# Two groups of four batches, re-laid expert weights and a folded local gate in a two-layer kernel

## The chip, the cores and the metric

The kernel runs on one core of a Trainium2 chip. The time is that of the device for one execution, in microseconds (us). The five engines are named as in the profile: PE (TensorE, with its weight loads as PEld), DVE (VectorE), ACT (ScalarE), POOL (GpSimd) and SP (SyncE, which here only issues transfers).

## The reference, cut to what matters

Eight batches of 512 tokens, 128 channels wide, go through two layers. Each layer adds an attention and a mixture of experts to its input.

```python
xn = layernorm(x)
x = x + L0_attn(xn) + L0_ffn(xn)        # states of two key sets; 8 experts, the best one
xn = layernorm(x)
x = x + L1_attn(xn) + L1_ffn(xn)
```

Layer 0's attention forms for each of two key and value projections a state over all tokens, `einsum('kbhnd,kbhne->kbhde', ks, vs)`, multiplies the two states, and applies the queries to the product.

Layer 1's attention has a local part (windows of 32 keys and the 32 before, 16 heads) and a remote part (64 latents), each with a gate that depends on the query:

```python
base = (j > i) & (j <= i + W)            # i: query in its block, j: key in its window of 64
sc = where(mask, einsum(Qb, Kw) / sqrt(D), -inf)
local = einsum(softmax(sc), Vw)
gl = sigmoid(einsum('bhsd,hd->bhs', Q, gate_local_w))
gr = sigmoid(einsum('bhsd,hd->bhs', Q, gate_remote_w))
out = (gl * local + gr * rem) @ w_out
```

By `base`, key 0 of a window is seen by no query.

Layer 1's experts send each token to two of eight:

```python
logits = x_flat @ gate_w.T
topk_probs, topk_idx = top_k(softmax(logits), 2)
hidden = relu(einsum('th,ehf->tef', x_flat, w1) + b1)   # F = 512
y = einsum('tef,efh->teh', hidden, w2) + b2
y_flat = sum(gathered(y, topk_idx) * topk_probs)
```

## The kernel before

All work is float32. Every product has therefore two instructions ("passes") on PE. A batch is 4 tiles of 128 tokens.

*Stages.* `layer0(b)` (line 756) does layer 0 for a batch and also projects `v` and the logits of layer 1. `attention1(b)` (line 923) is layer 1's attention. `route(h)` (line 1152) sorts the tokens of a group of batches by expert; `experts1(h)` (line 1309) runs the experts over the group's tiles; `output(b)` (line 1431) fetches the expert rows back and adds them.

*Groups.* `GROUPS = (2, 3, 3)` at line 34 says how many batches share a routing. Each token counts twice, and each expert's rows are rounded up to tiles of 128, so a group of n batches has `_tiles(n)` = (1024 n + 1016) // 128 tiles at most, all of which are run: 23, 31 and 31.

*An expert tile.* SP loads `w1`, `w2` (256 KB each) and `b2` of the tile's expert. POOL gathers its 128 rows from DRAM (`xgt`), PE transposes them (`tpx`), four products give `hp` (line 1405), ACT adds the bias and applies relu (`ht`), four products give `yp`, DVE adds `b2` (`ys`) and POOL scatters the rows (`y_rows`, line 1371). The bias comes out of a small product of `b1r` (line 580) with the one-hot expert of each tile.

*Layer 0's experts.* The gate of each token is written to DRAM as `gd` and read back for each expert, broadcast to all partitions (`gbc`, line 704); DVE and POOL in turn multiply it with the input (`xg`), and PE sums eight products into `rp`.

*Layer 0's states.* For each key set, `hk` (line 822) is a sum of four products with the keys as the stationary operand; ACT copies it, PE transposes it (`tph`), ACT copies that to `hT`.

*Layer 1's local part.* Queries of four heads at a time are spread into `qe`, keys lie in `kT` (line 939) with 32 zeros ahead, and a product for each block and each four heads gives scores against a window of 64 keys (`sc`, line 1076). For each pair of score banks ACT copies the past keys to `m`, DVE lays the seen own keys over it (predicated copy), then maximum (`amx`), difference, exponential, sum (`asd`), reciprocal (`ard`, line 1110) and the division follow, a transpose (`pt`), two masks (`pw`), and the products into `pv`. The gates come from two 512-column products (`gj`) and two tanh into `gsb` (line 988); the local one is applied in `loc` (line 1139), and POOL adds it to `aT`.

*The order.* No engine call is issued where it stands. A `Recorder` (line 126) collects every operation with an estimated duration (`_duration`, line 395) and with its dependencies; `order` (line 238) then places them on the engines' timelines, by rank, and each engine's instructions are issued in that order. The ranks come from `PLAN` (line 1461), a start and an end for every stage and batch, found by the authors and written out by hand. `_fill` (line 349) puts bf16 products of zeros into pauses that the plan expects on PE. All recorded operations carry the line of the recorder's call, 389, so the profile tells them apart by tile names.

Of the kernel before, what the change touches and what calls it, by code (L numbers as in the profile page):

```python
# [33 lines left out]
GROUPS = (2, 3, 3)  # L34
# [39 lines left out]
def _constants():  # L74

    c = np.zeros((P, _CN), np.float32)
    p = np.arange(P)

    def put(name, a):
        lo, hi = _CCOL[name]  # L80
        c[: a.shape[0], lo:hi] = a.reshape(a.shape[0], hi - lo)

    put("ident", np.eye(P))

    less = np.eye(P)
# [12 lines left out]
    g = np.arange(P // CHUNK)  # L98
    late = np.zeros((P, P), np.float32)
    group = np.zeros((P, P), np.float32)  # L100
    for at in (0, LC):
        late[at : at + len(g)] = np.where(p[None, :] % len(g) > g[:, None], NEG, 0.0)
        group[at : at + len(g)] = p[None, :] // CHUNK == g[:, None]
    put("late", late)
    put("group", group)
    put("first", np.broadcast_to(E - np.arange(E), (P, NT, E)))
    put("before", p[:, None] < p[None, :])
    put("iota", np.broadcast_to(p, (P, P)))
    put("part4", p[:, None] // NFC)
    put("chunk4", p[:, None] % NFC == np.arange(NFC)[None, :])  # L110
    put("within", p)
    n = 2 * max(GROUPS) * NT
    put("tile", np.broadcast_to(1 + np.arange(n), (P, n)))
    return c


class Op:
# [4 lines left out]
        "missing", "opens", "claims", "index", "follows", "shape", "last", "room",  # L122
# [3 lines left out]
class Recorder:  # L126
# [8 lines left out]
    PAUSE, FILL = 0.6, 0.8  # L135
    filled = 0
# [23 lines left out]
    def add(self, engine, emit, writes, reads, time, delay, shape=None):  # L160
# [12 lines left out]
        op = Op()  # L173
        op.engine, op.emit, op.time, op.delay = engine, [emit], time, delay
        op.shape = op.last = shape
        op.index, op.follows = len(self.ops), ()
        op.uses = uses
        self.ops.append(op)
# [59 lines left out]
    def order(self):  # L238
# [26 lines left out]
        free = dict.fromkeys(("PE", "DVE", "ACT", "POOL", "SP"), 0.0)  # L265
        shape = None
# [7 lines left out]
        while len(out) < len(self.ops):  # L274
# [47 lines left out]
            free[e] = op.end  # L322
            for t in uses.get(op.index, ()):
                left[t.name] -= 1
                holders[t.name] = max(holders.get(t.name, 0.0), op.end + op.delay)
                if not left[t.name]:
                    slots[t.tag].append(holders[t.name])
            for other in op.before:
                lag = op.delay
# [39 lines left out]
class _Engine:  # L369
# [3 lines left out]
    def __getattr__(self, method):  # L373
# [3 lines left out]
        def record(*args, **kwargs):  # L377
# [6 lines left out]
            if name == "tensor":  # L384
                rows = aps[1].shape[0]
                cols = int(np.prod(list(aps[1].shape)[1:])) if method == "matmul" else P
                shape = (rows, 32 * ((cols + 31) // 32))
            r.add(
                r.ENGINES[name], lambda: call(*args, **kwargs), aps[:1], aps[1:], time, delay, shape  # L389
# [5 lines left out]
def _duration(engine, method, aps):  # L395
# [6 lines left out]
    if "dma" in method:  # L402
        size = 4e-6 * int(np.prod(list(aps[0].shape)))
        return (1.25, 2.4) if engine == "gpsimd" else (0.5, 2.0 + 5.0 * size)
# [18 lines left out]
    if method == "reciprocal":  # L423
# [5 lines left out]
        0.095 + (0.28 if len(aps) == 4 and (n == P or n < 8) else 0.0)  # L429
# [6 lines left out]
def two_layers_kernel(  # L436
# [52 lines left out]
    experts_row = work.tile([1, E * C], F32, tag="gsb", name="experts_row", bufs=1)  # L489
# [66 lines left out]
    wgl = const.tile([P, 2, P], F32, name="wgl")  # L556
    nc.vector.tensor_scalar_mul(wgl[:, 0], ct("heads"), wt("gl"))
    nc.vector.tensor_scalar_mul(wgl[:, 1], ct("heads"), wt("gr"))
# [18 lines left out]
    nc.gpsimd.memset(vb, 0.0)  # L577

# [31 lines left out]
    nc.scalar.copy(b1r, b1p[: E * NFC, :P])  # L610
# [103 lines left out]
    for h, n in enumerate(GROUPS):  # L714
# [17 lines left out]
        "hk": "w2",  # L732
# [23 lines left out]
    def layer0(b):  # L756
# [77 lines left out]
        hT = tile(work, [P, 2, C], "hT", "hT" + nm)  # L834
        nc.scalar.copy(hT, tp[:, : 2 * C].rearrange("p (k c) -> p k c", c=C))
# [75 lines left out]
    wgl1 = const.tile([P, 2, P], F32, name="wgl1")  # L911

    def gates_of_input():
# [6 lines left out]
        mm(wp[:, : 2 * P], wqT, wgl.rearrange("p k c -> p (k c)"))  # L920
        nc.scalar.copy(wgl1.rearrange("p k c -> p (k c)"), wp[:, : 2 * P])

    def attention1(b):
# [64 lines left out]
        gsb = work.tile([P, 2, N], F32, tag="gsb", name="gsb" + nm, bufs=1)  # L988
# [63 lines left out]
        nc.vector.scalar_tensor_tensor(aT, gsb[:, 1, :], 1.0, rem_p, ALU.add, ALU.mult)  # L1052
# [21 lines left out]
        for hf in range(2):  # L1074

            four = [bank(f"sc{nm}_{hf}{r}") for r in range(4)]
            with nc.together(0.31):
                for j in range(8):
                    blk = 8 * hf + j
                    for r in range(4):  # L1080
# [228 lines left out]
    def experts1(h):  # L1309
# [6 lines left out]
        def fetch(j):  # L1316
# [29 lines left out]
            for move, to in ((load_first, first), (load_second, second), (load_third, third)):  # L1346
                nc.add("SP", move, [to], [], 0.55, 3.3)
                nc.ops[-1].follows = (fetch.last,)
# [17 lines left out]
        def scatter(j, ys):  # L1366
# [8 lines left out]
            nc.add("POOL", store, [], [ys, ids], 1.25, 2.4)  # L1375
# [21 lines left out]
        for j in range(TILES + 1):  # L1397
            if j < TILES:
# [53 lines left out]
    def load_next(b):  # L1452
        xs[b] = load_x(b)
        if b == 1:
# [13 lines left out]
        "attention1": (  # L1468
            (33, 150), (148, 194), (204, 270), (284, 611),
            (549, 789), (924, 1084), (1023, 1271), (1198, 1498),  # L1470
        ),
        "experts1": ((68, 410), (427, 1006), (967, 1293)),
        "output": (
            (676, 701), (627, 663), (1181, 1203), (995, 1107),
            (1262, 1379), (1408, 1425), (1456, 1524), (2493, 2506),
# [80 lines left out]
```

## Time and profile before

| | |
|---|---|
| median of 8 runs | 616.31 us (613.77 to 618.62) |
| the profiled execution | 616.91 us |
| its span, first to last instruction | 614.9 us |
| mean granted TensorE clock | 0.965 |
| DMA bytes moved | 91.63 MB, 106,532 packets |
| expert tiles | 85 |

A row of a profile names an engine, the operation, the tile that it writes and those it reads, with the shape, the count, the busy time, the mean of one, and the idle time of the engine ahead of it with what ended that. Busy time of overlapping instructions is counted once.

### The profile page before, as it was taken

How to read it: one execution, taken by the hardware profiler on the slowest of the kernel's cores; microseconds unless marked ns; L12 is line 12 of the kernel's file. 1: busy time of each engine (PE TensorE's matmuls, PEld its weight loads, DVE VectorE, ACT ScalarE, POOL GpSimd, SP SyncE). 2: the span in 40 equal slices, each digit the busy share in tenths (PEclk: the TensorE clock that was granted, in tenths of full speed). 3: DMA queues.
4: the chain of work that ended last, by engine and by line, in shares of the span. 5: the costliest groups of instructions: out<-in, count | busy, mean ns of one | idle time of the engine just before them, and what ended most of it. 6: DMA issues, size and time to landing. Idle time of an engine off the chain costs nothing.

```text
span 614.9 us, 15660 instructions
## 1 busy us (share of the span) xinstructions
PE 550.3 (89%) x5487; PEld 455.0 (74%) x5487; DVE 478.1 (78%) x1297; ACT 343.3 (56%) x950; POOL 402.8 (66%) x422
## 2 busy tenths in 40 slices
PE   9989888889989899879998979987998999999893
PEld 3478577679778578757987868987777888888842
DVE  2796899988979889997866868789843773965695
ACT  3623737653856775445677438454585468557620
POOL 3045134689578738844776877887778898887562
PEclk9999999889999999989997989989999999999988
DMA  5045053454352345435664557667866777897122
GB/s 159 22 131 159 14 157 85 111 176 133 87 155 61 102 135 144 119 69 168 189 182 111 176 170 228 166 182 200 236 199 179 215 220 218 214 266 207 60 86 70
DMA packets 106532, 91.63 MB, mean 149 GB/s; under 512 B 8940, under 2 KB 84086, under 8 KB 106454
## 3 DMA queue, kind: packets, MB, share of 16 engines
q1 hardware_dynamic: 100582, 78.41, 44.4%
q0 software_dynamic: 5440, 11.15, 6.9%
q10 hardware_dynamic: 432, 1.07, 0.5%
q8 instruction: 44, 0.72, 0.5%
q14 instruction: 34, 0.28, 0.1%
HBM read 80.70 MB, written 9.90 MB: 147 GB/s over the span
## 4 chain that ended last, share of the span: by engine, by line
DVE 33%; PE 27%; POOL 14%; DMA 9%; issue 8%; ACT 8%; SPq 0%; DVEq 0%; POOLq 0%; ACTq 0%
PE hp L389 4%; PE yp L389 4%; DMA gbc<-gd 4%; POOL m L389 4%; PE rp L389 3%; DVE pw L389 3%; POOL y_rows L1371 3%; POOL xgt L389 3%; DVE xg L389 2%; DVE m L389 2%; ACT vb L389 2%; PE pv L389 2%; POOL pw L389 2%; DVE x L389 2%; DMA w<-in_w_dram 2%
## 5 line engine op out<-in xcount | busy, mean ns | idle before, releaser
L389 ACT ACTIVATE ht<-hp,bias 128x128 f32<-128x128 f32 x340 | 101.2, 372 | 43.5 <-PE hp L389 42.4
L1371 POOL DMA_INDIRECT y_rows<-ys,row_i x85 | 89.2, 1049 | 41.6 <-issue 9.6
L389 POOL DMA_INDIRECT xgt<-x_rows,token_i x85 | 87.5, 1030 | 23.0 <-issue 17.8
L389 PEld LDWEIGHTS hp<-xt,w 128*128 128x128 f32 x680 | 85.4, 196 | 13.5 <-issue 6.3
L389 PE MATMUL hp<-xt,w 128*128 128x128 f32 x680 | 92.6, 282 | 2.1 <-DVE ys L389 1.0
L389 PE MATMUL yp<-w,ht 128*128 128x128 f32 x680 | 91.3, 279 | 1.4 <-ACT ht L389 1.4
L389 PEld LDWEIGHTS yp<-w,ht 128*128 128x128 f32 x680 | 83.7, 193 | 6.5 <-ACT ht L389 3.0
L389 PE MATMUL rp<-we_sb,xg 128*128 128x128 f32 x512 | 67.9, 281 | 3.9 <-POOL xg L389 2.6
L389 PEld LDWEIGHTS rp<-we_sb,xg 128*128 128x128 f32 x512 | 62.4, 194 | 9.6 <-POOL xg L389 5.3
L389 POOL TENSOR_TENSOR xg<-xT,gbc 128x512 f32<-128x512 f32 x32 | 42.9, 1341 | 36.7 <-DMA gbc<-gd 23.7
L389 PE MATMUL pv<-pw,vb 128*32 128x64 f32 (+1 forms) x1088 | 38.0, 230 | 14.4 <-POOL pw L389 11.4
L389 PEld LDWEIGHTS pv<-pw,vb 128*32 128x32 f32 x1088 | 34.4, 120 | 21.6 <-POOL pw L389 17.2
L389 POOL TENSOR_TENSOR pw<-pt,csb 128x512 f32<-128x512 f32 x32 | 42.4, 1326 | 3.6 <-DVE pt L389 3.3
L389 ACT ACTIVATE m<-m,zero_b 128x512 f32<-128x512 f32 x32 | 23.1, 722 | 38.2 <-POOL m L389 38.1
L389 DVE TENSOR_TENSOR pw<-pt,csb 128x512 f32<-128x512 f32 x32 | 42.9, 1340 | 0.3
L389 POOL TENSOR_TENSOR m<-m,ard 128x512 f32<-128x512 f32 x32 | 34.1, 1066 | 13.0 <-DVE ard L389 7.0
L389 POOL TENSOR_TENSOR le<-le,lrd 128x128 f32<-128x128 f32 (+3 forms) x32 | 23.9, 753 | 25.9 <-DVE lrd L389 18.7
L389 POOL TENSOR_TENSOR m<-m,amx 128x512 f32<-128x512 f32 x32 | 33.8, 1064 | 10.1 <-DVE amx L389 9.2
L389 ACT COPY vb<-v 32x128 f32<-32x128 f32 x128 | 37.7, 295 | 1.8
L389 PE MATMUL sc<-kT,qe 32*128 32x64 f32 x1024 | 36.8, 282 | 1.0 <-DVE k L389 0.6
L389 PEld LDWEIGHTS sc<-kT,qe 32*128 32x128 f32 x1024 | 33.8, 194 | 4.4 <-DVE k L389 1.1
L389 DVE COPY_PREDICATED m<-csb,sc 128x256 f32<-128x256 int32 x64 | 25.2, 433 | 14.9 <-POOL m L389 12.0
(261 smaller groups left out, 1214.8 us busy)
## 6 DMA issues: line engine op xcount, KB each, us to landing
w<-in_w_dram SPq DMA_DIRECT2D x170, 256.0 KB
gbc<-gd SPq DMA_DIRECT2D x64, 256.0 KB
b<-in_experts_b_dram SPq DMA_DIRECT2D x85, 64.0 KB
yg<-y_rows SPq DMA_DIRECT2D x16, 256.0 KB
x<-in_x_dram SPq DMA_DIRECT2D x8, 256.0 KB
x_rows<-xn SPq DMA_DIRECT2D x8, 256.0 KB
out_dram<-x SPq DMA_DIRECT2D x8, 256.0 KB
xgt<-x_rows,token_i POOLq DMA_INDIRECT x85, 3.3
```

Of the source, the lines that this page charges most:

```text
L389: r.ENGINES[name], lambda: call(*args, **kwargs), aps[:1], aps[1:], time, delay, shape
L1371: tc.nc.gpsimd.indirect_dma_start(views[j], bass.IndirectOffsetOnAxis(ap=ids, axis=0), ys, None)
```

## The change

Nothing of the result changes. There are five parts.

1. Groups of four: two routings instead of three, 39 tiles each. The planner's ranks (`PLAN`) are new throughout.
2. The planner gives each transfer a share of a common DMA timeline: its data lands no sooner than the transfers before it allow, plus 1.5 us. Some estimates change with it (a POOL transfer's delay, small DVE operations).
3. `w2` of an expert is laid out so that a partition holds four neighbouring rows. The hidden units of chunk k are then k, k+4, k+8 and so on; `hp` reads `w1` at that stride, and `b1r` is brought to the same order by a write to DRAM and four loads.
4. The local gate: `kT` holds for each block its own window of two blocks, and in the column of the unseen key 0 stands the gate's weight. The score product then yields the gate's logit in that column; a tanh on ACT takes it (`gz`), and DVE multiplies it into the reciprocal. The mask that clears that key in `pw` is as before.
5. States turned: the products take the input as stationary and both key sets as moving operand, so that no transposes are needed.

```diff
-GROUPS = (2, 3, 3)
+GROUPS = (4, 4)
...
-    put("part4", p[:, None] // NFC)
-    put("chunk4", p[:, None] % NFC == np.arange(NFC)[None, :])
+    put("part4", p[:, None] % E)
+    put("chunk4", p[:, None] // E == np.arange(NFC)[None, :])
...
+            op.lag = op.delay
+            if op.traffic:
+                carried = max(carried, op.end) + op.traffic
+                op.lag = max(op.lag, carried + self.LANDING - op.end)
...
+                rate = 2.6 if len(aps[0].shape) == 2 and aps[0].shape[1] >= 512 else 3.3
+                traffic = rate * 4e-6 * int(np.prod(list(aps[0].shape)))
...
-    wgl = const.tile([P, 2, P], F32, name="wgl")
-    nc.vector.tensor_scalar_mul(wgl[:, 0], ct("heads"), wt("gl"))
-    nc.vector.tensor_scalar_mul(wgl[:, 1], ct("heads"), wt("gr"))
+    wgl = const.tile([P, P], F32, name="wgl")
+    nc.vector.tensor_scalar_mul(wgl, ct("heads"), wt("gr"))
...
-    nc.scalar.copy(b1r, b1p[: E * NFC, :P])
+    b1t = work.tile([E * NFC, P], F32, tag="pt", name="b1t", bufs=1)
+    nc.scalar.copy(b1t, b1p[: E * NFC, :P])
+    b1d = dram.tile([E, FF], F32, tag="b1d", name="b1d", bufs=1)
+    nc.sync.dma_start(b1d.rearrange("e (c p) -> (e c) p", p=P), b1t)
+    for k in range(NFC):
+        nc.sync.dma_start(
+            b1r[k * E : (k + 1) * E], b1d.rearrange("e (p k) -> k e p", k=NFC)[k]
+        )
...
-        h3 = hp[:, : 2 * C].rearrange("p (k c) -> p k c", c=C)
-        for k in range(2):
-            for t in range(NT):
-                mm(
-                    h3[:, k], ks[:, t, (k + 1) * C : (k + 2) * C], xn[:, t],
-                    start=t == 0, stop=t == NT - 1,
-                )
-        hk = tile(work, [P, 2, C], "hk", "hk" + nm)
-        nc.scalar.copy(hk, h3)
-        tp = bank("tph" + nm)
-        for k in range(2):
-            nc.tensor.transpose(tp[:, k * C : (k + 1) * C], hk[:, k], ident)
+        for t in range(NT):
+            mm(hp[:, : 2 * C], xn[:, t], ks[:, t, C:], start=t == 0, stop=t == NT - 1)
         hT = tile(work, [P, 2, C], "hT", "hT" + nm)
-        nc.scalar.copy(hT, tp[:, : 2 * C].rearrange("p (k c) -> p k c", c=C))
+        nc.scalar.copy(hT, hp[:, : 2 * C].rearrange("p (k c) -> p k c", c=C))
...
-        kT = work.tile([P, W + N], F32, tag="kT", name="kT" + nm, bufs=1)
-        nc.scalar.copy(kT[:, W:], pj)
-        nc.vector.memset(kT[:, :W], 0.0)
+        kT = work.tile([P, NB, 2, W], F32, tag="kT", name="kT" + nm, bufs=1)
+        kb3 = pj.rearrange("p (b k) -> p b k", k=W)
+        nc.scalar.copy(kT[:, :, 1], kb3)
+        nc.scalar.copy(kT[:, 1:, 0, 1:], kb3[:, : NB - 1, 1:])
+        nc.vector.memset(kT[:, 0, 0, 1:], 0.0)
+        nc.vector.tensor_copy(kT[:, :, 0, 0], wt("gl").to_broadcast([P, NB]))
...
-        for k in range(2):
-            pj = bank(f"gj{nm}_{k}")
-            mm(pj, wgl1[:, k, :], x2)
-            nc.scalar.activation(gsb[:, k, :], pj, AF.Tanh, bias=zero, scale=0.5)
+        pj = bank("gj" + nm)
+        mm(pj, wgl1, x2)
+        nc.scalar.activation(gsb, pj, AF.Tanh, bias=zero, scale=0.5)
...
-                            kT[rows, blk * W : (blk + 2) * W],
+                            kT[rows, blk].rearrange("p a k -> p (a k)"),
...
+                gz = small.tile([P, 2, 8], F32, tag="gz", name=f"gz{u}")
                 for k in range(2):
+                    nc.scalar.activation(gz[:, k], parts[k][:, :, 0, 0], AF.Tanh, bias=zero, scale=0.5)
                     nc.scalar.copy(m[:, k], parts[k][:, :, 0])
...
                 nc.vector.reciprocal(rd, sd)
+                nc.vector.scalar_tensor_tensor(
+                    rd, gz.rearrange("p k j -> p (k j)"), 1.0, rd, ALU.add, ALU.mult
+                )
...
-        loc = work.tile([P, N], F32, tag="loc", name="loc" + nm, bufs=1)
-        nc.vector.scalar_tensor_tensor(loc, gsb[:, 0, :], 1.0, pv, ALU.add, ALU.mult)
-        nc.gpsimd.tensor_tensor(aT, aT, loc, ALU.add)
+        nc.vector.tensor_add(aT, aT, pv)
...
-                tc.nc.sync.dma_start(second, w2[e].rearrange("e (k p) c -> p (e k) c", p=P))
+                tc.nc.sync.dma_start(second, w2[e].rearrange("e (p k) c -> p (e k) c", k=NFC))
...
-            nc.add("POOL", store, [], [ys, ids], 1.25, 2.4)
+            nc.add("POOL", store, [], [ys, ids], 1.25, 2.4, traffic=0.22)
...
-                        hp[:, k * P : (k + 1) * P], ws[j][0][:, k * P : (k + 1) * P],
+                        hp[:, k * P : (k + 1) * P], ws[j][0][:, k::NFC],
...
     PLAN = {
...
         "layer0": (
-            (0, 1), (0, 10), (1, 39), (77, 134),
-            (121, 154), (178, 309), (241, 418), (313, 760),
+            (0, 42), (1, 89), (55, 98), (62, 187),
+            (135, 236), (217, 311), (292, 327), (303, 367),
         ),
-        "route": ((68, 100), (273, 384), (789, 901)),
+        "route": ((143, 210), (344, 374)),
...
-        "experts1": ((68, 410), (427, 1006), (967, 1293)),
+        "experts1": ((266, 448), (446, 892)),
```

More of the change, by code (lines that the diff above doesn't have):

```diff
@@ L121 @@
         "engine", "emit", "uses", "time", "delay", "rank", "after", "before", "start", "end",
-        "missing", "opens", "claims", "index", "follows", "shape", "last", "room",
+        "missing", "opens", "claims", "index", "follows", "shape", "last", "room", "traffic", "lag",
     )
@@ L135 @@
     PAUSE, FILL = 0.6, 0.8
+    LANDING = 1.5
     filled = 0
@@ L158, in together, with add @@
         self.group, self.share = None, 1.0
-    def add(self, engine, emit, writes, reads, time, delay, shape=None):
+    def add(self, engine, emit, writes, reads, time, delay, shape=None, traffic=0.0):
         uses = [(a, True) for a in writes] + [(a, False) for a in reads]
@@ L175, in add @@
         op.shape = op.last = shape
+        op.traffic = traffic
         op.index, op.follows = len(self.ops), ()
@@ L265, in order @@
         free = dict.fromkeys(("PE", "DVE", "ACT", "POOL", "SP"), 0.0)
+        carried = 0.0
         shape = None
@@ L322, in order @@
             free[e] = op.end
+            op.lag = op.delay
+            if op.traffic:
+                carried = max(carried, op.end) + op.traffic
+                op.lag = max(op.lag, carried + self.LANDING - op.end)
             for t in uses.get(op.index, ()):
                 left[t.name] -= 1
-                holders[t.name] = max(holders.get(t.name, 0.0), op.end + op.delay)
+                holders[t.name] = max(holders.get(t.name, 0.0), op.end + op.lag)
                 if not left[t.name]:
@@ L328, in order @@
             for other in op.before:
-                lag = op.delay
+                lag = op.lag
                 if other.engine == e and lag < 1.0:
@@ L387, in record @@
                 shape = (rows, 32 * ((cols + 31) // 32))
+            traffic = 0.0
+            if "dma" in method:
+                rate = 2.6 if len(aps[0].shape) == 2 and aps[0].shape[1] >= 512 else 3.3
+                traffic = rate * 4e-6 * int(np.prod(list(aps[0].shape)))
             r.add(
-                r.ENGINES[name], lambda: call(*args, **kwargs), aps[:1], aps[1:], time, delay, shape
+                r.ENGINES[name], lambda: call(*args, **kwargs), aps[:1], aps[1:], time, delay,
+                shape, traffic,
             )
@@ L403, in _duration @@
         size = 4e-6 * int(np.prod(list(aps[0].shape)))
-        return (1.25, 2.4) if engine == "gpsimd" else (0.5, 2.0 + 5.0 * size)
+        return (1.25, 3.0) if engine == "gpsimd" else (0.5, 2.0 + 5.0 * size)
     if engine == "tensor":
@@ L428, in _duration @@
     return (
-        0.095 + (0.28 if len(aps) == 4 and (n == P or n < 8) else 0.0)
+        0.095 + (0.28 if len(aps) == 4 and (n == P or n < 8) else 0.1 if n <= 16 else 0.0)
         + (0.0009 if fast else 0.0016 if both else 0.00102) * n,
@@ L488, in two_layers_kernel @@
     biases = work.tile([1, row_n], F32, tag="pw", name="biases")
-    experts_row = work.tile([1, E * C], F32, tag="gsb", name="experts_row", bufs=1)
+    experts_row = work.tile([1, E * C], F32, tag="pw", name="experts_row")
     def bias_row(name):
@@ L731, in two_layers_kernel @@
         "gT": "w2",
-        "hk": "w2",
         "hT": "xt",
@@ L909, in layer0 @@
         yield
-    wgl1 = const.tile([P, 2, P], F32, name="wgl1")
+    wgl1 = const.tile([P, P], F32, name="wgl1")
     def gates_of_input():
@@ L919, in gates_of_input @@
         wp = bank("wgp")
-        mm(wp[:, : 2 * P], wqT, wgl.rearrange("p k c -> p (k c)"))
-        nc.scalar.copy(wgl1.rearrange("p k c -> p (k c)"), wp[:, : 2 * P])
+        mm(wp[:, :P], wqT, wgl)
+        nc.scalar.copy(wgl1, wp[:, :P])
     def attention1(b):
@@ L987, in attention1 @@
             nc.scalar.copy(lat[:, 4 + i], pjs[i][:, : 2 * C])
-        gsb = work.tile([P, 2, N], F32, tag="gsb", name="gsb" + nm, bufs=1)
-        for k in range(2):
-            pj = bank(f"gj{nm}_{k}")
-            mm(pj, wgl1[:, k, :], x2)
-            nc.scalar.activation(gsb[:, k, :], pj, AF.Tanh, bias=zero, scale=0.5)
+        gsb = work.tile([P, N], F32, tag="gsb", name="gsb" + nm, bufs=1)
+        pj = bank("gj" + nm)
+        mm(pj, wgl1, x2)
+        nc.scalar.activation(gsb, pj, AF.Tanh, bias=zero, scale=0.5)
         yield
@@ L1051, in attention1 @@
             yield
-        nc.vector.scalar_tensor_tensor(aT, gsb[:, 1, :], 1.0, rem_p, ALU.add, ALU.mult)
+        nc.vector.scalar_tensor_tensor(aT, gsb, 1.0, rem_p, ALU.add, ALU.mult)
         yield
@@ L1344, in load_third @@
                 tc.nc.sync.dma_start(third, experts_b[e, 1].to_broadcast([P, C]))
-            for move, to in ((load_first, first), (load_second, second), (load_third, third)):
-                nc.add("SP", move, [to], [], 0.55, 3.3)
+            for move, to, traffic in (
+                (load_first, first, 0.67), (load_second, second, 0.67), (load_third, third, 0.22)
+            ):
+                nc.add("SP", move, [to], [], 0.55, 3.3, traffic=traffic)
                 nc.ops[-1].follows = (fetch.last,)
@@ L1463, in two_layers_kernel @@
         "layer0": (
-            (0, 1), (0, 10), (1, 39), (77, 134),
-            (121, 154), (178, 309), (241, 418), (313, 760),
+            (0, 42), (1, 89), (55, 98), (62, 187),
+            (135, 236), (217, 311), (292, 327), (303, 367),
         ),
-        "route": ((68, 100), (273, 384), (789, 901)),
+        "route": ((143, 210), (344, 374)),
         "attention1": (
-            (33, 150), (148, 194), (204, 270), (284, 611),
-            (549, 789), (924, 1084), (1023, 1271), (1198, 1498),
+            (56, 149), (190, 255), (223, 324), (306, 349),
+            (331, 488), (443, 520), (541, 880), (842, 1023),
         ),
-        "experts1": ((68, 410), (427, 1006), (967, 1293)),
+        "experts1": ((266, 448), (446, 892)),
         "output": (
-            (676, 701), (627, 663), (1181, 1203), (995, 1107),
-            (1262, 1379), (1408, 1425), (1456, 1524), (2493, 2506),
+            (433, 680), (733, 818), (885, 962), (766, 922),
+            (984, 1066), (916, 930), (916, 1001), (1433, 1552),
         ),
```

## The prediction

> **What bounds the kernel now.** I read the busy shares first, then the two stretches before and after the first expert product, then the rows of the parts that the diff touches, then the chain that ended last.
>
> ```profile
> span 614.9 us, 15660 instructions
> PE 550.3 (89%) x5487; PEld 455.0 (74%) x5487; DVE 478.1 (78%) x1297; ACT 343.3 (56%) x950; POOL 402.8 (66%) x422
> ```
>
> TensorE is busy 89% of the span, VectorE 78%. Neither alone sets the end everywhere, so I cut the run where the first group's routing lets its experts start. The index tile `row_i` ends a routing; `hp<-xt,w` is the first product of an expert tile.
>
> ```profile
> L389 DVE SCALAR_TENSOR_TENSOR row_i<-row,none x3: 184/191/192, 114.1 to 444.1; 128x31 int32<-128x31 f32 x2, 128x23 int32<-128x23 f32 x1
> ...
> L389 PEld LDWEIGHTS hp<-xt,w x680: 186/192/338, 125.9 to 575.7; 128*128 128x128 f32 x170
> L389 PE MATMUL hp<-xt,w x680: 272/275/582, 126.1 to 575.8; 128*128 128x128 f32 x170
> ...
> 0.00:126.10 126.10, 113.45 (x786) 79.43 (x787) 100.98 (x335) 65.11 (x153) 46.09 (x66) 0.97 0.36 104
> 126.10:614.90 488.80, 436.81 (x4703) 375.57 (x4702) 377.11 (x962) 278.21 (x797) 356.76 (x357) 0.96 0.57 161
> 0.00:114.10 114.10, 102.37 (x675) 71.73 (x676) 89.72 (x303) 59.60 (x143) 36.48 (x56) 1.00 0.38 110
> ...
> 100.00:200.00 100.00, 91.35 (x985) 76.67 (x983) 90.54 (x258) 60.63 (x158) 74.55 (x76) 0.95 0.44 124
> ```
>
> The columns of the windows are the stretch, its length, busy us of PE, PEld, DVE, ACT and POOL, the granted clock, the DMA share and GB/s. The reader should see: routing 0 ended at 114.1 us and experts began 12.0 us later; up to there VectorE was busy 89.7 us (0.786 of the time) and has little to wait for; after 126.1 us TensorE is busy 436.8 of 488.8 us (0.894), so that stretch is paced by TensorE. Between 100 and 200 us VectorE reaches 0.905: that is as dense as I have seen it.
>
> ```profile
> L389 ACT ACTIVATE ht<-hp,bias 128x128 f32<-128x128 f32 x340 | 101.2, 372 | 43.5 <-PE hp L389 42.4
> L389 PEld LDWEIGHTS hp<-xt,w 128*128 128x128 f32 x680 | 85.4, 196 | 13.5 <-issue 6.3
> L389 PE MATMUL hp<-xt,w 128*128 128x128 f32 x680 | 92.6, 282 | 2.1 <-DVE ys L389 1.0
> L389 PE MATMUL yp<-w,ht 128*128 128x128 f32 x680 | 91.3, 279 | 1.4 <-ACT ht L389 1.4
> ...
> L389 PE MATMUL gj<-x2p,wgl 128*128 128x512 f32 x32 | 16.9, 609 | 0.8 <-ACT gsb L389 0.8
> ...
> q1 hardware_dynamic: 100582, 78.41, 44.4%
> ```
>
> Matmuls overlap, so I price an instruction by busy time over count (92.6/680 = 0.136 us), not by its mean. PE hardly waits ahead of expert products (2.1 and 1.4 us): what an expert tile saves on PE is saved time.
>
> **The change part by part.**
>
> *Groups.* 23 + 31 + 31 = 85 tiles become 39 + 39 = 78. A tile's PE work is 8 x 0.136 + 8 x 91.3/680 + one transpose of 13.5/85 = 2.32 us; seven fewer save 16.3 us of PE, 28 x 101.2/340 = 8.3 us of ACT, 14 x 1.04 = 14.6 us of POOL (89.2/85 and 87.5/85) and 7 x 0.28 = 1.9 us of DVE. One of three routings goes, about 12 us of small DVE rows, but the other two have 32 columns where they had 16 to 24, which I put at +7: net -5.
>
> *Local gate.* One of two 512-column products a batch goes: 16.9/2 = 8.5 us of PE, and 8 x 0.689 = 5.5 us of ACT (tanh of `gsb`). POOL loses the add into `aT`, 8 x 1.275 = 10.2 us; DVE's `loc` (0.682) becomes an add of the same size. Added: 64 tanh of 128x8 on ACT, bounded by the 128x16 copy at 0.174 and the 128x12 activation at 0.304; I take 0.25, 16 us. 32 multiplies of 128x16 on DVE, between 0.184 (128x32 tensor-tensor) and 0.326 (`shifta`): I take 0.25, 8 us. The keys are copied twice: 8 x 0.58 = 4.6 us of ACT, and 8 small DVE copies, 1 us. The two tanh stand ahead of the `m` copies on ACT, so every score pair starts some 0.5 us later; DVE's predicated copy is queued behind. ACT is idle 44% of the span and expert products are in between; without that cover it is 32 x 0.5 = 16 us.
>
> *States turned.* The products keep their columns (16 passes of 128 become 8 of 256); two transposes go, 3.3 us of PE, and a copy, 8 x 0.376 = 3.0 us of ACT.
>
> PE sum: -16.3 - 8.5 - 3.3 = -28.1 us; about 1 us more goes with the third routing's products: -29. DVE +2, ACT +4, POOL -25.
>
> *Second weights.* A 256 KB load of `w2` is 512 packets now and 128 afterwards: with 7 tiles less, some 40,000 of 100,582 packets go. Waits on `w` are 2% of the chain, 12 us. Gain between 0 and 12; I take 2, since PE's own rows show under 2 us of waiting on `w`. For it `hp` reads its weights at every fourth column (`[:, k::NFC]`, 16 bytes apart). No row of the trace reads so. Nearest rows are the same load without stride: 192 ns median, 338 the slowest. So 0 to 146 ns for each of 78 x 8 = 624 loads, 0 to 91 us; a gain is excluded, as the same bytes are loaded. I take 0, as the row of the same operation and shape is the median one.
>
> [...]
>
> *First biases.* They are now turned by a trip through DRAM: one write and four loads of 8 rows x 128 elements, each of 4 bytes, that is 4,096 packets. A packet of queue 1 costs 0.444 x 614.9 x 16 / 100582 = 43 ns of one engine (at 780 bytes): 11 us over 16 engines, 22 if 8 rows keep each load to 8 engines. They follow ACT's copy (ends 14.8 us) and a write's landing (about 2 us, as `gd` at 26.4 to `gbc` at 28.3), are issued from 17 to 19 us and so end at 30 to 41 us; `gd` of batch 0 is queued behind them on SP, and the first `xg` ran at 33.05. Cost 0 to 15 us; I take 3.
>
> *Scheduler and plan.* They move everything. I priced the two instruction orders with the rows of the profile. PE work without the filler matmuls (bf16 zeros set into planned pauses): 538 us before, 94 ahead of the first `hp` and 444 behind; after 509, 160 and 349. Fillers go from 116 to 190, of them 70 to 135 ahead of the first `hp`: the early stretch, with four batches of layer 0 and over one of attention and no experts to fill pauses, is planned with more idle time. Priced DVE work ahead of `row_i` of group 0 is 199 against 114, so 199/114 x 89.7 = 157 us busy.
>
> First stretch: 157 us at a DVE share between 0.786 (as now) and 0.905 (as at 100 to 200 us) is 173 to 199 us; with 0.846, halfway, 185. Plus 12 to the first `hp` and 3 for the biases: 200. Second stretch: (349 + 55 x 0.25 of fillers) x 436.8/455 = 348 us of PE. At 0.894 it is 389 us; POOL and DVE are denser there (priced POOL 305 us, 0.78 against 0.73), so I take 0.88: 395. Sum: 200 + 395 - 2 = 593 of span, against 614.9. The profiled execution took 616.91, 2.0 more than its span, and lies 0.6 above the median of 616.31. Forecast 595.
>
> Bounds: 185 + 389 - 6 + 2 = 570 at the good ends; 211 + 15 + 348/0.865 (the share from 500 us on, 98.62 of 114) + 2 = 630 at the bad ends.
>
> **The rivals.**
>
> *The strided load decides (slower).* Place: the 624 `hp` loads. At present loads (85.4 us busy) and products (92.6) are level, so a longer load shows at once; PE is the bound in just that stretch. From (616.3 - 595)/624 = 34 ns a load the whole gain is gone; at 90 ns it is 595 + 56 = 651. For it: no cover. Against: only the worst clocked load of 680 was longer. Chance 0.15.
>
> *The empty first half takes the gain.* All experts are pushed behind 200 us; VectorE stays at 0.786, and the biases hold the gate of batch 0 the full 15 us: 211 + 15 + 395 + 2 - 2 = 621. For it: the fillers, and 13% of the first 60 us of the chain on `gbc<-gd`. Against: attention of batch 0 and 1 now lies between. Chance 0.12.
>
> *Transfers mattered more.* `gbc`, `w` and `y_rows` on the chain shrink with fewer packets: 575. Chance 0.06.
>
> **How the numbers follow.** The forecast (580 to 613 by itself) has 0.67. The range 579 to 630 takes in the second rival and leaves out most of the first and third. A difference under 0.3%, some 1.9 us, can't be told from none. Faster: 0.67 + 0.06 + 0.02 of the second rival = 0.75; same 0.05 and slower 0.05 from that rival, with 0.15 of the first: 0.20.
>
> **What would show it.** `hp` at 624 loads of 192 ns (right) or well above (first rival); the first `hp` at about 200 us; `gj` at 16 records; PE busy near 520 to 540 us; DVE near 480; first `xg` at 33 us, or later by the biases' packets; after the first `hp`, PE at 0.88. I am wrong if the first `hp` comes after 215 us, or the second stretch is above 405.

## The result and the profile after

The changed kernel takes 647.22 us (median of 17 runs, 643.85 to 653.09), the kernel before beside it 616.33: a ratio of 1.0504, 95% interval 1.0485 to 1.0522. It is 5% slower. The forecast was 595, so it missed by 52 us and on the wrong side.

The page of the changed kernel: span, busy shares, the chain that ended last, and the two costliest groups (busy time, mean of one, idle time ahead).

```profile
span 648.0 us, 15246 instructions
PE 604.8 (93%) x5340; PEld 509.1 (79%) x5340; DVE 469.4 (72%) x1276; ACT 342.7 (53%) x973; POOL 385.1 (59%) x400
...
PE 55%; DVE 21%; ACT 8%; POOL 7%; DMA 4%; issue 3%; POOLq 0%; SPq 0%; DVEq 0%; ACTq 0%
PE hp L402 19%; PE yp L402 9%; PE rp L402 4%; PE pv L402 4%; DMA gbc<-gd 3%; ACT ks L402 2%; PE sc L402 2%; DVE x L402 2%; ACT vb L402 2%; POOL m L402 2%; PE kp L402 2%; DVE ard L402 2%; PE rem_p L402 1%; DVE xg L402 1%; DVE asd L402 1%
...
L402 PE MATMUL hp<-xt,w 128*128 128x128 f32 x624 | 157.4, 397 | 0.0
L402 PEld LDWEIGHTS hp<-xt,w 128*128 128x128 f32 x624 | 152.0, 327 | 6.1 <-issue 2.9
```

The chain of the kernel before, to compare:

```profile
DVE 33%; PE 27%; POOL 14%; DMA 9%; issue 8%; ACT 8%; SPq 0%; DVEq 0%; POOLq 0%; ACTq 0%
PE hp L389 4%; PE yp L389 4%; DMA gbc<-gd 4%; POOL m L389 4%; PE rp L389 3%; DVE pw L389 3%; POOL y_rows L1371 3%; POOL xgt L389 3%; DVE xg L389 2%; DVE m L389 2%; ACT vb L389 2%; PE pv L389 2%; POOL pw L389 2%; DVE x L389 2%; DMA w<-in_w_dram 2%
```

TensorE was to fall from 550 us busy to 520 or 540; it rose to 605. `hp` alone went from 92.6 us for 680 passes to 157.4 for 624, and from 4% of the chain to 19%. The reason is in the durations, minimum, median and maximum in ns, of the two products that use the expert weights:

```profile
L402 PEld LDWEIGHTS hp<-xt,w x624: 307/329/333, 219.4 to 602.3; 128*128 128x128 f32 x156
L402 PE MATMUL hp<-xt,w x624: 272/397/500, 219.5 to 602.4; 128*128 128x128 f32 x156
L402 PEld LDWEIGHTS yp<-w,ht x624: 186/192/209, 224.7 to 606.0; 128*128 128x128 f32 x156
L402 PE MATMUL yp<-w,ht x624: 272/275/377, 224.7 to 606.1; 128*128 128x128 f32 x156
```

A weight load at every fourth column takes 329 ns (307 to 333); the load of `yp`, of the same shape without stride, still takes 192. This is what the first rival named, in the place that it named. A pass of `hp` now costs 157.4/624 = 0.252 us in place of 0.136, 72 us over 624 passes.

The windows tell the rest (stretch, length, busy us of PE, PEld, DVE, ACT, POOL, clock, DMA share, GB/s). The boundaries are the end of routing 0 and the first `hp`:

```profile
0.00:219.50 219.50, 197.66 (x1490) 139.27 (x1490) 178.53 (x549) 111.98 (x274) 93.43 (x110) 0.92 0.29 85
219.50:648.00 428.50, 407.12 (x3853) 369.84 (x3851) 290.90 (x728) 230.71 (x700) 291.70 (x291) 0.99 0.56 159
0.00:193.10 193.10, 174.32 (x1262) 122.84 (x1263) 154.84 (x481) 96.20 (x234) 75.89 (x93) 0.93 0.27 80
```

The first `hp` came at 219.5 us, not at 200, although routing 0 ended at 193.1. Behind it TensorE is busy 0.95 of the time, the mark of a longer product and not of waits. Two questions follow: how much of 72 us of longer products is time, and why the rest of the change saved nothing.

### The profile page after: what moved, and what is told of

It reads as the page before. It is cut to its first block, busy times and chain, and to the rows that moved or that the text cites. A ratio compares the mean times of both kernels' runs of the same rounds, so it can differ in the third digit from the quotient of the medians.

```text
span 648.0 us, 15246 instructions
## 1 busy us (share of the span) xinstructions
PE 604.8 (93%) x5340; PEld 509.1 (79%) x5340; DVE 469.4 (72%) x1276; ACT 342.7 (53%) x973; POOL 385.1 (59%) x400
## 4 chain that ended last, share of the span: by engine, by line
PE 55%; DVE 21%; ACT 8%; POOL 7%; DMA 4%; issue 3%; POOLq 0%; SPq 0%; DVEq 0%; ACTq 0%
PE hp L402 19%; PE yp L402 9%; PE rp L402 4%; PE pv L402 4%; DMA gbc<-gd 3%; ACT ks L402 2%; PE sc L402 2%; DVE x L402 2%; ACT vb L402 2%; POOL m L402 2%; PE kp L402 2%; DVE ard L402 2%; PE rem_p L402 1%; DVE xg L402 1%; DVE asd L402 1%
## 5 line engine op out<-in xcount | busy, mean ns | idle before, releaser
L402 PE MATMUL hp<-xt,w 128*128 128x128 f32 x624 | 157.4, 397 | 0.0
L402 PEld LDWEIGHTS hp<-xt,w 128*128 128x128 f32 x624 | 152.0, 327 | 6.1 <-issue 2.9
L402 ACT ACTIVATE ht<-hp,bias 128x128 f32<-128x128 f32 x312 | 91.9, 369 | 100.8 <-PE hp L402 100.5
L1391 POOL DMA_INDIRECT y_rows<-ys,row_i x78 | 82.5, 1058 | 63.2 <-DVE ys L402 30.6
L402 POOL DMA_INDIRECT xgt<-x_rows,token_i x78 | 77.5, 994 | 29.2 <-issue 16.5
L402 PE MATMUL yp<-w,ht 128*128 128x128 f32 x624 | 82.4, 277 | 1.4 <-DVE m L402 1.4
L402 PEld LDWEIGHTS yp<-w,ht 128*128 128x128 f32 x624 | 76.1, 193 | 3.9 <-DVE m L402 1.6
L402 DVE TENSOR_TENSOR ys<-yp,b 128x128 f32<-128x128 f32 x78 | 22.2, 286 | 64.7 <-PE yp L402 59.5
L402 POOL TENSOR_TENSOR le<-le,lrd 128x128 f32<-128x128 f32 (+3 forms) x32 | 23.6, 745 | 25.9 <-ACT m L402 12.7
L370 PEld LDWEIGHTS <-zeros 128*128 128x128 bf16 x190 | 18.9, 103 | 20.9 <-issue 3.7
L402 DVE TENSOR_TENSOR xg<-xT,gbc 128x512 f32<-128x512 f32 x32 | 30.7, 960 | 5.6 <-DMA gbc<-gd 3.7
```

Source lines behind the costliest of these rows:

```text
L370: self.nc.tensor.matmul(full, self.zeros[:, :parts], self.zeros.unsqueeze(1).to_broadcast([P, NT, P]), start=fresh, stop=fresh,)
L1391: tc.nc.gpsimd.indirect_dma_start(views[j], bass.IndirectOffsetOnAxis(ap=ids, axis=0), ys, None)
```

## The experiments

Theories were set against each other in turn. In the first four runs the *stride theory* (the longer weight load is the loss) stood against the *plan theory* (the loss comes of two groups, which have no expert tiles early on).

**e1: the third part undone.**

```diff
-                tc.nc.sync.dma_start(second, w2[e].rearrange("e (p k) c -> p (e k) c", k=NFC))
+                tc.nc.sync.dma_start(second, w2[e].rearrange("e (k p) c -> p (e k) c", p=P))
...
-                        hp[:, k * P : (k + 1) * P], ws[j][0][:, k::NFC],
+                        hp[:, k * P : (k + 1) * P], ws[j][0][:, k * P : (k + 1) * P],
```

> The changed kernel with its third part undone: the second weights as before (four runs of one row a partition), the first weights read column by column, the first biases without the trip through DRAM; every engine's order otherwise as in the changed kernel. Stride theory (a weight load at every fourth column takes 329 instead of 192 ns and the products wait for it: 157.4/624 = 252 ns a pass against 136): 624 x 0.116 = 72 us less, 575, between 568 and 590; the load back at 192 ns, the product at 136 ns a pass. Plan theory (two groups leave the first 220 us without experts and that is what costs; a longer load would only fill time that is empty anyway): 625 or more, with the busy time of the products lower but the end hardly moved.

**e2: four rows a partition kept, columns sorted in DRAM.** The arrays of `w1` and `b1` are handed over with their hidden units in the order that the chunks want.

```diff
-        "w1": np_["L1_ffn_w1"],
+        "w1": np_["L1_ffn_w1"].reshape(E, C, P, NFC).transpose(0, 1, 3, 2).reshape(E, C, FF),
...
-                        hp[:, k * P : (k + 1) * P], ws[j][0][:, k::NFC],
+                        hp[:, k * P : (k + 1) * P], ws[j][0][:, k * P : (k + 1) * P],
```

> The changed kernel, with the second weights still four rows a partition, but the first weights and biases stored in DRAM with their hidden units already in the order k, k+4, k+8, so that hp reads neighbouring columns and no trip of the biases is needed. Stride theory: like e1, 575, with a load of 192 ns; if fewer packets matter, 1 to 8 us below e1. A second theory, that four rows a partition in themselves slow the loads of PE (through the bytes' arrival): load above 250 ns and above 610. Plan theory: 625 or more.

**e3: the third part alone, in the kernel before.** The edit is e1's, the other way round, with the biases' trip through DRAM.

> The kernel before, with the third part alone: four rows a partition, hp at every fourth column, the biases through DRAM; groups, order, gate and states as before. Stride theory: 680 passes x 0.116 = 79 us more than before, 695, between 680 and 705. Plan theory: the kernel before keeps experts through the whole run and hides part of it; 616 to 640.

**e4: half the stride.**

```diff
-                        hp[:, k * P : (k + 1) * P], ws[j][0][:, k::NFC],
+                        hp[:, k * P : (k + 1) * P], ws[j][0][:, k // 2 * 256 + k % 2 : (k // 2 + 1) * 256 : 2],
```

> The changed kernel at half the stride: a partition of the second weights holds two runs of two neighbouring rows, hp reads every second column, 8 bytes apart, order as in the changed kernel. [...] If the load grows with the stride, it lies at about 238 ns (a third of the way) or more: 595 to 615. If any stride costs the same: 329 ns and 647.

Measured, with the kernel before at 615.71 beside them:

| run | us | ratio to before | interval |
|---|---|---|---|
| e1 plain columns | 617.96 | 1.0029 | 0.9999 to 1.0059 |
| e2 columns sorted | 617.15 | 1.0012 | 0.9977 to 1.0047 |
| e3 before, strided | 646.81 | 1.0483 | 1.0438 to 1.0527 |
| e4 stride two | 619.40 | 1.0058 | 1.0024 to 1.0091 |

The loads of `hp` in e2, e3 and e4:

```profile
L402 PEld LDWEIGHTS hp<-xt,w x624: 186/192/337, 213.4 to 569.3; 128*128 128x128 f32 x156
```

```profile
L389 PEld LDWEIGHTS hp<-xt,w x680: 307/329/347, 125.7 to 607.0; 128*128 128x128 f32 x170
```

```profile
L402 PEld LDWEIGHTS hp<-xt,w x624: 192/196/333, 213.2 to 573.4; 128*128 128x128 f32 x156
```

The stride is settled: with it, either kernel is some 30 us slower (647.2 against 618.0, and 646.8 against 615.7), without it the load is back at 192 ns. Eight bytes apart cost 4 ns a load, sixteen cost 137: the 196 ns of e4 are neither the 238 of a load that grows with the stride nor the 329 of any stride alike. Why the loss lies between the two, no run shows. The way the `w2` bytes arrive plays no part that the runs can tell (e1 and e2 are level, 617.96 and 617.15), and the biases' trip none (e4 has it, at 619.40).

Both theories missed the size. `hp` is busy for 157.4 us with the stride and for 87.4 in e2, 70 us more, and only some 30 of them are time (33 between the two profiled executions). About as much came out of pauses: TensorE's idle time falls from 72.7 us in e2 to 43.2 (88% busy to 93%). The last 8 us are other products that got shorter, with a higher granted clock (0.99 against 0.96 behind the first `hp`). And e1 and e2 at 617 leave 22 us to the forecast unexplained: the change without its stride is level with the kernel before.

**Where the saved products went.** The same two windows, with the fillers' own share of PE and PEld beside them, of e2 (first three lines, then fillers) and of the kernel before:

```profile
0.00:60.00 60.00, 55.41 (x300) 36.31 (x301) 38.27 (x138) 26.76 (x59) 19.61 (x34) 1.00 0.38 119
60.00:213.50 153.50, 134.42 (x1192) 97.90 (x1190) 139.80 (x410) 85.39 (x216) 74.34 (x77) 0.96 0.24 74
213.50:615.00 401.50, 352.59 (x3853) 307.38 (x3851) 300.07 (x730) 229.64 (x700) 290.56 (x291) 0.96 0.56 169
...
60.00:213.50 153.50, 20.24 (x76) 7.50 (x76) 0.96 0.24 74
213.50:615.00 401.50, 13.16 (x55) 5.07 (x55) 0.96 0.56 169
```

```profile
0.00:60.00 60.00, 55.27 (x307) 36.00 (x307) 39.37 (x136) 24.25 (x49) 17.89 (x33) 1.00 0.39 117
60.00:213.50 153.50, 137.45 (x1332) 110.37 (x1331) 137.88 (x396) 94.36 (x244) 96.70 (x100) 0.97 0.39 109
213.50:615.00 401.50, 357.53 (x3853) 308.63 (x3852) 300.83 (x766) 224.72 (x658) 288.26 (x291) 0.96 0.60 169
...
60.00:213.50 153.50, 4.27 (x16) 1.54 (x16) 0.97 0.39 109
213.50:615.00 401.50, 12.66 (x46) 4.60 (x46) 0.96 0.60 169
```

Take the fillers off PE. From 60 to 213.5 us the kernel before does 133.2 us of products, e2 does 114.2: 19 us less; 15.4 us of the kernel before are `hp` and `yp`, and e2 has no expert tile to run yet. Behind 213.5 both have about as much left, 344.9 and 339.4 us, and both need 401 us for it. The saving of 24 us is real, but 19 of it appear as an emptier stretch in the middle, in which 16 us more of fillers stand.

VectorE is 0.91 busy in that stretch, which suggested the *vector theory*: VectorE paces up to some 220 us. Its rival, the *TensorE theory*, says that what leaves TensorE leaves the time. (In the kernel before VectorE is as dense there, 137.9/153.5 = 0.90.) Four runs let the planner re-order around a changed piece of work.

> The kernel before with parts four and five alone (local gate in the unseen key's column, states turned), groups of 2, 3 and 3 and their ranks as before, all weights and biases laid as before; the planner re-orders with the new operations. Vector theory (up to some 220 us VectorE paces, 0.91 busy, behind it TensorE): TensorE loses 11.8 us of products and transposes, VectorE gains 15.1 us of gate multiplies and 3 of key copies; experts run from 126 us on and take the room: 608 to 618. TensorE theory (what leaves TensorE leaves the time): 616 - 11.8 = 604, between 600 and 607. If the gate's longer way through ACT and VectorE decides: 620 or more.

> The kernel with two groups and columns sorted (e2: 617.2), with the local gate as before: two 512-column products and the multiply at the end, POOL's add. TensorE has 8.5 us more, VectorE some 18 less, POOL 10 more; the planner re-orders. Vector theory: the gain on VectorE in the first stretch and the loss on TensorE in the second about cancel: 612 to 622. TensorE theory: 617 + 8.5 = 626.

```diff
-            nc.vector.tensor_scalar_mul(
-                qe[:, :, hl, :], pj.rearrange("p (b q) -> p b q", q=W), head4[:, hl : hl + 1]
-            )
+            nc.scalar.activation(
+                qe[:, :, hl, :], pj.rearrange("p (b q) -> p b q", q=W), AF.Identity,
+                bias=zero, scale=head4[:, hl : hl + 1],
+            )
```

> e2 (617.2), with the 32 copies that spread the queries to their heads moved from VectorE (22.5 us in all, 2.8 a batch) to ACT (some 20 us, ACT being busy 56%); the planner re-orders. Vector theory: the part of it ahead of 300 us, four to five batches, is 11 to 14 us of VectorE where it paces, so first hp comes 4 to 8 us sooner than at 213.5 and the time is 603 to 611. TensorE theory: unchanged, 615 to 620.

> The kernel before with part five alone (states turned). TensorE 3.3 us less, ACT 3.0 less, a copy and two transposes less in the chain of each batch. Both theories: 610 to 616; nothing on VectorE is added, so under the vector theory it should be no worse than f1, under the TensorE theory 8 us worse than f1.

They ran beside a kernel before that takes 642.16 us at a lower granted clock (0.94 to 0.96, not about 0.97), so only ratios count: f1 1.0329 (1.0227 to 1.0431), f2 1.0408 (1.0311 to 1.0506), f4 1.0236 (1.0137 to 1.0335), f5 1.0302 (1.0212 to 1.0393). Neither theory had it. A gate whose longer way decides, which f1 named as a third case, would allow f1 (620 or more), but f5 has no part of the gate, only takes work away, and is 3% slower too. What all four share is that the planner found other orders.

**g1, g2, p1, p2: the order by itself.** g1 is e2 again, g2 f4 again, now side by side; p1 and p2 each change one estimate of the planner in the kernel before and no operation but the fillers (115 and 119 in place of 116). The edit of p1:

```diff
-            return 0.13, 0.2
+            return 0.12, 0.2
```

> The kernel of e2 again (two groups, gate and states as in the changed kernel, columns sorted), so that it stands beside the next one on one chip: its ratio to the kernel before was 1.001 on the first chip. Both theories: 0.99 to 1.01 on any chip; if the ratio differs by 2% or more, a chip with a lower granted clock shifts the two kernels unlike.

> The kernel of f4 again (g1 with the query copies on ACT), beside g1. Vector theory: 1 to 2% faster than g1, and fewer us up to the first hp. TensorE theory: equal to g1. If the order that the planner happens to find counts for more than the moved work: slower than g1 although VectorE has 22 us less to do.

> The kernel before with not one operation changed; only the planner's estimate of a transpose is 0.12 in place of 0.13 us, which changes the order (and the number of filler products) on every engine. Work theories: within 0.5% of the kernel before. Order theory (the ranks written out by hand were found for exactly one set of estimates, and any other order is worse): 1 to 4% slower, as f5, which removes work and came out 3% slower.

> As p1, by another estimate: the fixed part of an ACT copy 0.09 in place of 0.08 us. Work theories: within 0.5% of the kernel before. Order theory: 1 to 4% slower, by another amount than p1.

With 642.88 for the kernel before: g1 0.9978 (0.9944 to 1.0012), so e2 is level with it beside these runs too; g2 1.025 (1.0216 to 1.0283), 2.7% slower than g1 with 22.9 us of copies moved off VectorE; p1 1.011 (1.0078 to 1.0142) and p2 1.011 (1.0079 to 1.0141). So the same work in another order is 1.1% slower, some 7 us. The f runs therefore say little of their own edits: their effects are not told apart from that of the order, and part four and part five have no measured price of their own here. That the order alone makes the 3% of f5 is not shown: p1 and p2 show 1.1%.

This was measured only in the two batches of runs (f, then g and p) beside which the kernel before takes 642 us, and their traces differ from the rest. All eight profiled runs of f, g and p have waits that the profile can only put down to "another core or an unknown queue"; the other twelve runs have none. g1 and e2 are the same kernel. g1 reaches the first `hp` at 211.9 us, e2 at 213.5, and their mean clocks are 0.957 and 0.961; but g1's span is 633.6 us against 615.1, and all that it loses it loses behind 370 us. Its chain:

```profile
PE 37%; DVE 27%; ACT 11%; POOL 9%; issue 7%; DMA 4%; another core or an unknown queue 3%; POOLq 0%; SPq 0%; DVEq 0%; ACTq 0%
```

3% are 19 us, as much as g1 is longer; in the other seven chains the share is 1% or less. What makes these runs longer stays open, and whether another order costs 1.1% where the kernel before takes 616 us was not run.

The second part can be read without a run: with the transfers' shares set to zero, the planner puts out the same instructions in the same order as for e2, line for line. Counting what transfers share decides nothing in this kernel; the estimates that changed with it are not covered by that.

**h1 to h3: e2's own order, work taken out or added.** The planner sees the old work; only what is issued differs. The first edit is h1's, the second h2's.

```diff
+        for op in nc.ops[-5:]:
+            op.emit = []
```

```diff
         mm(pj, wgl1, x2)
+        if b < 3:
+            nc.ops[-1].emit += 4 * nc.ops[-1].emit[-1:]
```

> The kernel of e2 in its own order, but five VectorE operations of 192 elements a batch in layer 0 are not issued: the second refining step of the inverse norm is left out (40 operations, some 15 us of VectorE, all ahead of 350 us). e2 stands at 0.998 to 1.001 of the kernel before. Vector theory: 1.3 to 2.4% faster than e2, so 0.976 to 0.987 of the kernel before, and the first hp some 8 to 10 us sooner. TensorE theory: within 0.4% of e2.

> e2 in its own order, with the 512-column gate product of batches 0, 1 and 2 (at 64, 142 and 174 us) issued five times over in place of once: 12 x 1.06 = 12.7 us of TensorE added where VectorE is 0.91 busy. Vector theory: 0 to 4 us more, at most 0.6%. TensorE theory: 11 to 13 us more, 1.8 to 2.1%.

> As h2, but for batches 5, 6 and 7 (behind 400 us, where VectorE is 0.63 to 0.74 busy and TensorE 0.90): the same 12.7 us. Vector theory: TensorE paces here, 8 to 13 us more, 1.3 to 2.1%, clearly more than h2. TensorE theory: 11 to 13, equal to h2.

With 615.67 for the kernel before: h1 0.9967 (0.9931 to 1.0003), h2 1.0143 (1.0078 to 1.0209), h3 1.0132 (1.007 to 1.0193). e2 itself was measured at 0.9978 and 1.0012, in other batches of runs. The vector theory falls. 13.9 us of VectorE work taken out (478.1 to 464.2 busy) give 0.1 to 0.5% over e2, far from 1.3, and the first `hp` comes 2.0 us sooner, not 8 to 10. 12.7 us of TensorE work put into the stretch where VectorE is 0.91 busy cost as much as late: 7 to 10 us over e2, by intervals of about 4 us either way. The first `hp`, at 213.5 in e2, is at 221.8 in h2:

```profile
L402 PE MATMUL hp<-xt,w x624: 272/275/422, 221.8 to 580.1; 128*128 128x128 f32 x156
```

So VectorE alone does not pace the early stretch. The added work on PE, which stands in the chain of a batch, is paid for there too, at 0.6 to 0.8 of its size. That no other single engine paces it is not shown.

**i1 to i3: the fillers.** One theory was left: that the 74 fillers more of e2 (190 against 116) took up what the products saved.

```diff
+        if op.start > 60.0:
+            return
         for _ in range(int(self.FILL * op.room / 0.25)):
```

> e2 in its own order, without the fillers that are planned behind 60 us (135 of 198; some 33 us of TensorE). Filler theory (on the chip they stand in the way of ready products, and took up the saved TensorE time): 10 to 25 us faster than e2, 0.96 to 0.985 of the kernel before. Pause theory (they run where TensorE would wait anyway, because with no experts before 213 us there is nothing to issue): within 0.5% of e2; if the granted clock sinks without them, up to 2% slower.

> The kernel before in its own order, without the 62 fillers that are planned behind 60 us (some 17 us of TensorE). Filler theory: 3 to 10 us faster. Pause theory: within 0.5%, or slower if the clock sinks.

> The kernel before in its own order, with h1's edit: the second refining step of the inverse norm left out, 15 us of VectorE. h1 gave 0.3% on the two-group kernel. If layer 0's chain binds the early stretch of the two-group kernel more than that of the kernel before: nothing here, 0.998 to 1.002. If VectorE work is worth the same in both: 0.995 to 0.998.

With 615.35 for the kernel before: i1 1.0133 (1.0051 to 1.0214), i2 1.0071 (1.0042 to 1.01), i3 0.9961 (0.9934 to 0.9988). On balance fillers are no loss: without them both kernels are slower. The window of i1 that answers e2's:

```profile
60.00:213.50 153.50, 126.91 (x1095) 97.44 (x1094) 135.58 (x401) 83.61 (x209) 72.11 (x76) 0.86 0.24 74
```

The granted clock there sinks from 0.96 to 0.86, and the mean of the run from 0.961 to 0.928. The runs do not separate the two effects: a filler that stood in the way of a product could be outweighed by the clock. But the 22 us are not to be had by leaving fillers out. i3, which leaves out a refining step, is the only kernel that was measurably below the kernel before, by 0.4%; no kernel with the whole computation was.

## Why the prediction was wrong

**The step that failed first: "I take 0" for the strided load.** The bounds were right (0 to 146 ns a load; measured 137), and the choice between them was wrong. I took the median of the same operation without stride as the nearest row, but a row that does not read so says nothing of a stride. The load cost 137 ns more and the kernel some 30 us. The rival named the place: it gave 651 us at 90 ns a load, and the kernel took 647 at 137. That these lie so near is luck: its arithmetic charged every ns, which at 137 makes 595 + 85 = 680; in fact 70 us of longer products made 30 us of time.

**The first stretch: 200 us, measured 213.5 in e2.** Routing 0 ended at 187.4 in e2; 185 was worked out, from 157 us of VectorE (measured 154.7) at a share of 0.846 (measured 0.826), so that term held. The 12.0 us from there to the first `hp` were taken over from the kernel before and became 26.1; the 3 us for the biases are not in e2. What is queued on TensorE ahead of `hp` differs: in e2 it is attention and layer 0 of other batches, with which TensorE is busy for 22.3 of the 26.1 us. PE between those two events in e2 (start, duration, what, and in brackets the idle time ahead):

```profile
201.30 1.99 PE L402 MATMUL sc<-kT,qe 32*128 32x64 f32 x58 [1.26 <-DVE k L402]
203.22 0.66 PE L402 MATMUL tpd<-csb,xn 128*128 128x128 f32 x4
205.36 2.05 PE L402 MATMUL qj<-x2p,wsb 128*128 128x512 f32 x2 [1.48 <-DVE pm L402]
207.20 1.73 PE L402 MATMUL kj<-x2p,wsb 128*128 128x512 f32 x2
...
212.15 0.60 PE L402 MATMUL tpx<-csb,xgt 128*128 128x128 f32 x4
...
213.46 0.79 PE L402 MATMUL hp<-xt,w 128*128 128x128 f32 x5
```

POOL's gathers for the first four tiles (`xgt`) are spread between its other work as well, but the fourth was issued by 197.7 us:

```profile
196.74 0.98 POOL L402 DMA_INDIRECT xgt<-x_rows,token_i  x1 [0.16 <-DVE mvd L402]
```

A gather lands 2.8 to 6.9 us after its issue in e2 (median 3.6), so these rows were there at least 7 us before PE came to transpose them at 212.15. The step was costed as a fixed delay and is a place in the queues, TensorE's above all. In the profiled execution of the changed kernel another 6 us lie at the very start, where the clock was halved from about 12 to 24 us (0.50 in its windows). e4, with the same biases' trip, has its first `hp` at 213.2, and the other executions of the changed kernel have mean clocks of 0.965 to 0.981, this one 0.964; so this most likely belongs to that execution.

**The second stretch: 395 us, measured 401.5 in e2.** The share of 0.88 held: 352.6/401.5 = 0.878. The busy time was 352.6 instead of 348. The term was right within 2%.

**The second weights: a gain of 2 us.** e1 and e2 are level, although e2 moves 29,952 packets fewer on queue 1 (64,918 against 94,870), so no gain shows. From the kernel before (100,582) to e2 35,664 packets go, not some 40,000.

Together: 595 + 13.5 + 6.5 + 2 + 30 for the stride = 647.

**What held.** PE without fillers was to fall by 29 us: 518.4 to 494.0, that is 24. The biases' trip costs next to nothing: e4, which has it, is 1 to 2 us above e1 and e2, together with what a stride of two costs. It was charged 3. The gate multiply on VectorE is 15.1 us (12.8 in e2), not 8: its median is 172 ns but some took up to 2,154.

**The second rival** (the empty first half takes the gain) was half right, at a chance of 0.12: e1 and e2 end at 618 and 617, where it said 621, and the gain does go into the first half. Its mechanism did not hold: VectorE is at 0.826 up to the end of routing 0, not 0.786, and e1 and e2 have no trip of the biases to wait for. That the numbers are near is luck in part. The emptiness is TensorE's: 114.2 us of products in 153.5, where the kernel before has 133.2.

**Not settled.** How much of the lost 22 us belongs to two groups and how much to the ranks that were found for them: no run has one without the other, since new ranks are another order, and another order alone moved the time by 1% where it was measured.

## What to carry to other kernels

A cheaper transfer that made a matrix product read its weights at a stride of 16 bytes was paid for on TensorE at once (329 ns a load in place of 192, the kernel at 647 us in place of 617); sorting the bytes in DRAM (192 ns) or a stride of 8 (196 ns, 619 us) avoided it. Saved work did not count where nothing else was ready to take its place (19 of the 24 us became an emptier stretch): compare real work, fillers left out, in the same stretch of both profiles before booking a saving. In a kernel whose order is planned from estimates, first run the same work in another order (1.1% slower in p1 and p2); an edit whose effect is below that spread has not been measured.

## What was not expected of the hardware

The penalty of the stride comes nearly all between steps of 8 and 16 bytes: 192, 196 and 329 ns at 4, 8 and 16 (e2, e4 and the changed kernel; 12 was not run). One kernel takes 616 us in some batches of runs and 642 in others, with granted clocks of about 0.97 and 0.95. The clock does not account for it: g1 and e2 differ by 18.5 us with 0.957 and 0.961. Nor is it tied to the chip's number on record: chip 0 stands beside 642.16 in the f runs and beside 615.67 in the h runs. And 4,096 packets of 4 bytes, issued by 23.4 us, were done by about 25.5 us, less than the 30 to 41 that I had worked out from the mean packet.
